# Attention with a prompt part on one core: whole copies of the Gram matrix, maxima ahead of a transpose, finishing pieces spread, another order at the end, and the prompt projection two stages later

## The chip, the cores and the metric

The kernel runs on one core of a Trainium2 chip. The metric is the device time of one execution in microseconds (us). Beside it there is one profiled execution, whose trace shows every instruction of the five engines: TensorE (PE, matmuls; PEld is its loading of weights), VectorE (DVE), ScalarE (ACT), GpSimd (POOL), and SyncE (SP), which in this kernel issues nearly all transfers. All times below are counted from the start of the profiled span.

## The reference

Eight batches of 112 queries attend to 375 context rows each: 371 rows of text and 4 of a prompt. There are 20 heads of 16 channels, and the context has 512 channels.

```python
q = heads(hidden_states @ W_q)                     # 8, 20, 112, 16
k_t, v_t = heads(text_ehs @ W_k), heads(text_ehs @ W_v)
probs_t = softmax(einsum('bhsd,bhtd->bhst', q, k_t) * Dh ** -0.5)
text_out = einsum('bhst,bhtd->bhsd', probs_t, v_t)
k_ip, v_ip = heads(ip_ehs @ W_k_ip), heads(ip_ehs @ W_v_ip)
attn_scores = einsum('bhsd,bhnd->bhsn', q, k_ip) * Dh ** -0.5
qsem = l2norm(einsum('bhst,bte->bhse', probs_t, text_ehs))
sem = einsum('bhse,bne->bhsn', qsem, l2norm(ip_ehs))
probs_ip = softmax(attn_scores + 0.5 * sem) * spatial_mask
ip_out = einsum('bhsn,bhnd->bhsd', probs_ip, v_ip)
out = (text_out + ip_out) @ W_out + b_out + hidden_states
```

The costly part is qsem: per batch and head a row of 371 probabilities times the context of 512 channels, of which only the length and four inner products are used.

## The kernel before, in words

**The idea.** The length of qsem comes from the Gram matrix G of the context, the inner products of all its rows: the squared length is p G p for a row p of (unnormed) probabilities. G is symmetric, so only the part above the diagonal is kept, doubled, with the diagonal halved. To the right of G stand the inner products with the prompt, a column of ones and the values of a head, so one chain of products p x [G, prompt, ones, values] gives all that a head needs.

**Steps.** A batch has five groups of four heads. A step is one group of one batch, 40 in all; `steps[n]` is the n-th. Four heads run beside each other, each in 32 rows of TensorE. Behind the first step (`alone`), the steps of the first seven batches go in pairs (n, n + 1) for odd n: `pair(n)` does the products of both, `behind(n + 1)` the TensorE work that belongs to other batches. Scores are two steps ahead (`LEAD`). The last batch has a loop of its own and then `ending`.

**One step.** `scores` (L681) makes the scores of a head in a PSUM bank. `probabilities` takes the maximum of each row on VectorE (L694, tile nmx), the exponential on ScalarE (L698, tile p), copies four prompt scores (L700, ipl), and has SP copy p into xg in the order that the transpose needs (L705). `transposed` turns xg with VectorE (L717) into xgT: a half takes six of the twelve blocks of 32 context rows, and the halves are separate instructions where a stage asks for them. `product` (L729) runs the twelve blocks; block j goes into the columns from 32 j on, so the chain gets shorter. The last blocks of the first step of a pair are mixed with the first block of the second. `reduced` (L782, VectorE) multiplies the result with p and sums, `value_sums` (L756, ScalarE) copies the rest.

**The Gram matrix.** `gram` (L501) makes G of a batch in three chunks of 128 context rows, in a PSUM bank each. The four column tiles p of TensorE take one block of 32 rows each; `DEAL[c]` says which block q tile p takes in chunk c, and block q starts at column 32 q, as the part left of it isn't needed. For each chunk there are four matmuls (e = 0..3) in each tile. `doubled` copies a chunk to the tile ug with ScalarE, times two: one instruction for the columns that all tiles have (L477) and three for what a tile has more (L481). GpSimd then multiplies 128 columns with a mask (L482) that has zeros, halves and ones; the masks follow `DEAL`. The first batch has another way, `first_gram`, with `doubled_whole`, one copy for a chunk. `gram_to_groups` has SP copy ug four times to the tile u of the batch (L515, four transfers for each of four blocks), `values_to_dram` and `values_to_groups` bring the values through DRAM to the tile vr (L591, L600), and `placed` copies the 64 value columns of a group into u with GpSimd (L647), three copies for a step, one for each chunk. The products of the next step wait for these.

**Buffers and queues that matter here.** The tile u has two buffers, for even and odd batches. The weights of the prompt (wip, L110) are loaded into a tile with the same tag, so that the u of batch 1 takes the place of wip. An engine works through its instructions in order, and so does SP's queue: a transfer that waits for its data or its place holds up all behind it. Pools with a `tag` give out buffers in turn.

**The prompt projection.** `prompt_projections` has three pieces: 32 short matmuls of all prompts with wip (L274), three ScalarE copies and one of GpSimd to the tile kv (L282 to L285); then three transposes of kv (L290), a copy to kip (L293) and three VectorE products to kipb (L295); then two transfers to vipd (L305). Before, the first piece lies in `behind(0)`, the second at the start of `behind(2)` and the third at its end.

**Finishing a batch.** `finish(b)` is a generator with pieces, which `f(b, n)` runs n at a time from the stages of the next two batches: (0) the largest of ss and a bound, (1) square root on ScalarE and 1/z, with `divided` on GpSimd, (2) the fused logits fu and their maxima (VectorE, L840 to L846), (3) their exponential (ScalarE, L850), (4) sums and the weights w (VectorE, L854 to L858), (5) the prompt's part wv on GpSimd (L864 to L871), (6) transposes of the result (TensorE L876, ScalarE L880), (7) the output product (L885) and its transfer. `ending` does the same for the last batch, which nothing hides, in smaller pieces (L898 on); the last batch's loop runs pieces of batch 6 (`before`) between its own.

**What sets the order.** TensorE, VectorE and SP follow the order in which the code issues instructions (`manual_schedule`); ScalarE's and GpSimd's instructions are placed by the scheduler in the main part.

## Time and profile before

| | us |
|---|---|
| runs, median of 3 | 417.56 |
| lowest and highest | 415.61, 419.80 |
| the profiled execution's own time | 415.55 |
| its span in the trace | 413.7 |
| TensorE's clock granted | 1.0 in all 40 slices |

The profiled execution lies 1.85 us above its span: that is what a launch adds around the traced instructions. It lies with the lowest of the three runs. A row of the timeline reads: start, duration, engine, line of the kernel, operation, tile written <- tiles read, shape, how many instructions are taken together; in brackets, the idle time of the engine before it and what ended that time. A row of a group reads: line, engine, operation, shapes, count, then busy time in us, the mean of one in ns, and the idle time ahead of it.

### The profile page before, as it was taken

To read this page: it belongs to the slowest core of one execution; us is meant where nothing else is said; L and a number is where in the kernel's file an instruction comes from. 1 tells how busy PE (TensorE), PEld (TensorE's weight loads), DVE (VectorE), ACT (ScalarE), POOL (GpSimd) and SP (SyncE) were. 2 spreads that over 40 slices of the span, in tenths; PEclk is the share of its full clock that TensorE was granted. 3 is DMA by queue.
4 is the path that set the end of the run, shared out by engine and by line. 5 is a ranking of instruction groups with operands and counts; after the bars stand their busy time and mean duration, and the time that the engine had idled before them with its cause. 6 is when DMAs were issued, how large, how long until landed. Compare 5 with 4: busy or idle time off the path is not lost.

```text
span 413.7 us, 14175 instructions
## 1 busy us (share of the span) xinstructions
PE 406.8 (98%) x5627; PEld 322.1 (78%) x5627; DVE 327.7 (79%) x700; ACT 199.3 (48%) x715; POOL 114.8 (28%) x271
## 2 busy tenths in 40 slices
PE   8999999999999999999999999999999999999996
PEld 7867777788778786879686877779787878687884
DVE  4256787877988877887898897897798897878975
ACT  3255342346443852535553664334733484336763
POOL 4203211121351351021170045002034126004671
PEclk9999999999999999999999999999999999999999
DMA  8877965976584846667676666566856344668320
GB/s 235 168 198 230 197 170 144 205 189 174 130 188 117 189 120 172 157 145 175 165 160 134 169 157 158 141 171 151 186 149 164 95 123 128 159 162 197 97 53 28
DMA packets 58244, 64.64 MB, mean 156 GB/s; under 512 B 19061, under 2 KB 52041, under 8 KB 58180
## 3 DMA queue, kind: packets, MB, share of 16 engines
q1 hardware_dynamic: 57150, 61.47, 61.0%
q0 software_dynamic: 464, 1.56, 1.6%
q8 instruction: 44, 0.72, 0.8%
q10 hardware_dynamic: 566, 0.72, 0.5%
q14 instruction: 20, 0.16, 0.1%
HBM read 19.03 MB, written 5.22 MB: 59 GB/s over the span
## 4 chain that ended last, share of the span: by engine, by line
PE 97%; POOL 1%; issue 0%; ACT 0%; DVE 0%; POOLq 0%
PE ps_qd L729 45%; PE ps_v L566 13%; PE ps_k L527 10%; PE ps_g L501 8%; PE ps_s L681 7%; PE ps_q L361 3%; PE ps_o L885 3%; PE ps_k L544 3%; PE ps_g L460 1%; PE ps_w L447 1%; PE ps_a L876 1%; PE ps_c L430 1%; PE ps_q L343 1%; PE ps_x L332 0%; PE ps_o L981 0%
## 5 line engine op out<-in xcount | busy, mean ns | idle before, releaser
L729 PE MATMUL ps_qd<-u,xgT 32*112 32x40 f32 (+11 forms) x3840 | 218.3, 352 | 1.1 <-POOL u L647 1.0
L729 PEld LDWEIGHTS ps_qd<-u,xgT 32*112 32x112 f32 x3840 | 181.4, 172 | 34.3 <-issue 5.5
L717 DVE STREAM_TRANSPOSE xgT<-xg 128x768 f32<-128x768 f32 (+1 forms) x63 | 123.4, 1977 | 10.4 <-DMA xg<-p 8.6
L698 ACT ACTIVATE p<-ps_s,nmx 112x371 f32<-112x371 f32 x160 | 86.0, 585 | 55.5 <-DVE nmx L694 54.1
L694 DVE TENSOR_REDUCE nmx<-ps_s 112x1 f32<-112x371 f32 x160 | 77.5, 536 | 32.9 <-PE ps_s L681 30.9
L647 POOL COPY u<-vr 128x64 f32<-128x64 f32 x120 | 26.9, 238 | 204.8 <-PE ps_qd L729 118.9
L782 DVE CUSTOM_DVE_ANT_0 p<-ps_qd,p 112x371 f32<-112x371 f32 x152 | 73.2, 536 | 12.9 <-ACT pvs L756 8.3
L681 PE MATMUL ps_s<-kT,qm 32*112 32x375 f32 (+1 forms) x320 | 62.0, 486 | 0.0
L566 PE MATMUL ps_v<-wv_sb,ctxT 128*128 128x320 f32 x192 | 56.1, 439 | 0.3 <-ACT kT L534 0.3
L756 ACT COPY pvs<-ps_qd 112x21 f32<-112x21 f32 x152 | 21.8, 197 | 55.7 <-DVE ss L782 49.2
L566 PEld LDWEIGHTS ps_v<-wv_sb,ctxT 128*128 128x128 f32 x192 | 35.3, 190 | 14.7 <-ACT kT L534 1.2
L527 PE MATMUL ps_k<-ctxT,wk_sb 128*128 128x371 f32 x128 | 43.6, 484 | 0.0
L527 PEld LDWEIGHTS ps_k<-ctxT,wk_sb 128*128 128x128 f32 x128 | 23.0, 190 | 13.2 <-issue 1.3
L681 PEld LDWEIGHTS ps_s<-kT,qm 32*112 32x112 f32 x320 | 28.5, 171 | 5.9 <-ACT ug L481 0.4
L501 PE MATMUL ps_g<-ctxT 128*32 128x375 f32 (+11 forms) x672 | 32.6, 334 | 0.0
L501 PEld LDWEIGHTS ps_g<-ctxT 128*32 128x32 f32 x672 | 27.9, 110 | 5.4 <-issue 2.0
L418 DVE STREAM_TRANSPOSE ctxT<-ct 128x512 f32<-128x512 f32 x21 | 22.2, 1069 | 6.1 <-DMA ct<-in_ctx_dram 6.1
L573 ACT COPY vext<-ps_v 128x320 f32<-128x320 f32 x24 | 10.2, 426 | 34.9 <-PE ps_v L566 33.9
L700 ACT COPY ipl<-ps_s 112x4 f32<-112x4 f32 x140 | 24.2, 173 | 0.0
L534 ACT COPY kT<-ps_k 128x371 f32<-128x371 f32 x16 | 7.5, 469 | 22.6 <-PE ps_k L527 22.3
L482 POOL TENSOR_TENSOR ug<-ug,half 128x128 f32<-128x128 f32 (+1 forms) x21 | 9.3, 450 | 30.7 <-ACT ug L481 30.7
L864 POOL TENSOR_TENSOR wv<-vip,w 112x1280 f32<-112x1280 f32 (+1 forms) x8 | 17.5, 2183 | 0.0
(153 smaller groups left out, 318.8 us busy)
## 6 DMA issues: line engine op xcount, KB each, us to landing
xg<-p SPq DMA_DIRECT2D x159, 162.3 KB
u<-ug SPq DMA_DIRECT2D x128, 99.0 KB
ct<-in_ctx_dram SPq DMA_DIRECT2D x28, 176.0 KB
vip<-vipd SPq DMA_DIRECT2D x7, 560.0 KB
vr<-vd SPq DMA_DIRECT2D x20, 120.0 KB
vd<-vext SPq DMA_DIRECT2D x7, 160.0 KB
out_dram<-ob SPq DMA_DIRECT2D x7, 140.0 KB
vr<-vd SPq DMA_DIRECT2D x12, 80.0 KB
```

What stands on the lines that cost most here:

```text
L418: nc.vector.transpose(ctxT[:, :, c * P : (c + 1) * P].rearrange("p e (j i) -> p j e i", i=RG), ct[:, some, :].rearrange("p j (k e) -> p j ...
L501: nc.tensor.matmul(ps[p * RG : (p + 1) * RG, q * RG : T - t0], ctxT[:, e, t0 + q * RG : t0 + (q + 1) * RG], ctxT[:, e, t0 + q * RG : T], s ...
L527: nc.tensor.matmul(ps[:, :TT], wk_sb[:, e, i * P : (i + 1) * P], s["ctxT"][:, e, :TT], start=(e == 0), stop=(e == NE - 1),)
L566: nc.tensor.matmul(ps[:, :C], ctxT[:, e, c * P : (c + 1) * P], wv_sb[:, e, :], start=(e == 0), stop=(e == NE - 1),)
L647: nc.gpsimd.tensor_copy(region(b, c)[:, :, UV - c * P :], s["vr"][:, c * QN : (c + 1) * QN, g, :])
L681: nc.tensor.matmul(ps[:S, :w], qm[a * RG : (a + 1) * RG, i, r, j * S : (j + 1) * S], s["kT"][a * RG : (a + 1) * RG, i, :w], start=True, st ...
L694: nc.vector.tensor_reduce(nmx, ps[:S, :TT], AX.X, ALU.max, negate=True)
L698: nc.scalar.activation(p, ps[:S, :TT], AF.Exp, bias=nmx)
L700: nc.scalar.copy(s["ipl"][:, groups[g][a], :], ps[:S, TT:T])
L717: nc.vector.transpose(xT[:, j : j + n].rearrange("p j (k q) -> p q j k", q=QN), xg[:, :, j * RG : (j + n) * RG].rearrange("p q (j k) -> p ...
L729: nc.tensor.matmul(banks[a][:S, j * RG : UW], xT[a * RG : (a + 1) * RG, j, :S], region(b, c)[a * RG : (a + 1) * RG, p, q * RG :], start=(j ...
L782: nc.vector.tensor_tensor_reduce(out=p, in0=ps[:S, :TT], in1=p, scale=1.0, scalar=0.0, op0=ALU.mult, op1=ALU.add, accum_out=s["ss"][:, h : ...
```

## The change

Five edits, in one diff.

1. *Whole copies.* `DEAL` gets other values for chunks 1 and 2. For batches 1, 2, 4 and 6 (`left_out` is false for their chunks 1 and 2) the matmuls of e = 0 in these chunks are made as wide as the chunk, and `doubled` then copies the chunk with one ScalarE instruction in place of four; what it copies more is zeroed by the mask. Chunk 0, and batches 3, 5 and 7, stay as they were, but for the dealing. The transfers of values to DRAM keep their number and change their sizes with the dealing.
2. *Maxima ahead.* In `pair(5)`, as in `pair(1)` before, the first half transpose of the second step comes behind the maxima of the coming step; `behind(4)` leaves it out.
3. *Finishing spread.* For odd batches, `behind` of group 1 runs pieces 1, 2 and 3 of `finish` at three places, and `pair` of group 2 runs 4 and 5. So fu and its maxima come ahead of the first half transpose on VectorE, and the sums and w, which came ahead of the next maxima, behind them.
4. *End order.* In the last batch's loop the scores for group 4 are issued one at a time after blocks 0 and 1, then two; pieces of batch 6's finish come at other places: GpSimd's first half of wv ahead of the shared products of group 2, both sums into attn ahead of the last batch's division, and TensorE's transposes of batch 6 ahead of those of batch 7.
5. *Prompt projection.* Its first piece moves from `behind(0)` to the start of `behind(2)`, which now runs it, the x transposes of `q`, the second piece, and then keys, half transpose, `q` and values. `behind(0)` makes two chunks of values in place of one, `behind(2)` one fewer.

Instructions: TensorE and SP have the same count of matmuls and transfers, ScalarE has 24 copies fewer.

```diff
--- before.py
+++ after.py
@@ -69,7 +69,7 @@
     assert (H, D, NC, NT, P) == (20, 16, 3, 3, 128) and RG == 2 * D
 
 
-    DEAL = ((0, 1, 2, 3), (3, 2, 0, 1), (1, 2, 3, 0))
+    DEAL = ((0, 1, 2, 3), (3, 1, 2, 0), (2, 3, 0, 1))
 
     def dealt(b, c):
         return DEAL[c] if b > 0 else DEAL[0]
@@ -465,15 +465,15 @@
                         stop=(e == NE - 1),
                     )
                 if c == NT - 1:
-                    doubled_whole(banks[r], r)
+                    doubled(banks[r], r, 0)
                 yield
 
-    def doubled(ps, c, deal=DEAL[0], h=0):
+    def doubled(ps, c, h, deal=()):
 
         t0 = c * P
         k = min(P, TT - t0)
         g = ug[:, GCOL[c] : GCOL[c] + T - t0]
-        common = (QN - 1) * RG
+        common = (QN - 1) * RG if deal else 0
         nc.scalar.mul(g[:, common:], ps[:, common : T - t0], 2.0)
         for p, q in enumerate(deal):
             if q < QN - 1:
@@ -481,13 +481,8 @@
                 nc.scalar.mul(g[own, q * RG : common], ps[own, q * RG : common], 2.0)
         nc.gpsimd.tensor_tensor(g[:, :k], g[:, :k], half[:, h, :k], ALU.mult)
 
-    def doubled_whole(ps, c):
-
-        t0 = c * P
-        k = min(P, TT - t0)
-        g = ug[:, GCOL[c] : GCOL[c] + T - t0]
-        nc.scalar.mul(g, ps[:, : T - t0], 2.0)
-        nc.gpsimd.tensor_tensor(g[:, :k], g[:, :k], half[:, 0, :k], ALU.mult)
+    def left_out(b, c):
+        return c == 0 or b > 1 and b % 2 == 1
 
     def gram(b):
 
@@ -498,14 +493,16 @@
             ps = bank(f"ps_g_{b}_{c}")
             for e in range(NE):
                 for p, q in enumerate(DEAL[c]):
+
+                    s0 = q * RG if e > 0 or left_out(b, c) else 0
                     nc.tensor.matmul(
-                        ps[p * RG : (p + 1) * RG, q * RG : T - t0],
+                        ps[p * RG : (p + 1) * RG, s0 : T - t0],
                         ctxT[:, e, t0 + q * RG : t0 + (q + 1) * RG],
-                        ctxT[:, e, t0 + q * RG : T],
+                        ctxT[:, e, t0 + s0 : T],
                         start=(e == 0),
                         stop=(e == NE - 1),
                     )
-            doubled(ps, c, DEAL[c], c)
+            doubled(ps, c, c, DEAL[c] if left_out(b, c) else ())
             yield
 
     def gram_to_groups(b, blocks):
@@ -1129,6 +1126,8 @@
 
     inputs = {7: (3, 5), 17: (5, B)}
 
+    late = (1, 5)
+
     def pair(n):
 
         one, two = steps[n], steps[n + 1]
@@ -1144,7 +1143,7 @@
                 coming_scores(n + LEAD, heads, tags[j])
                 coming_probabilities(n + LEAD, heads)
             if j == 1:
-                if n == 1:
+                if n in late:
                     transposed(*two, 0, BLK // 2)
                 transposed(*two, BLK // 2, BLK)
             if j % QN == QN - 1:
@@ -1168,7 +1167,7 @@
         if b % 2 and g in (0, NG - 1):
             f(b - 1 - (g == 0))
         if g in (1, 2):
-            f(b - 1, 3 - g)
+            f(b - 1, 2)
         reduced(b, g)
         value_sums(b, g)
 
@@ -1231,9 +1230,7 @@
             if n:
                 gr(nb, 2)
                 f(b - 1)
-            v(nb)
-            if n == 0:
-                run(("pp",), prompt_projections)
+            v(nb, 1 + (n == 0))
             if n:
                 tr(1)
                 f(b - 1, 2)
@@ -1244,11 +1241,16 @@
             turn[:] = ["qd"] * (6 + (b == 0)) + ["mm"]
             gram_to_groups(nb, (2,))
             if b == 0:
+                run(("pp",), prompt_projections)
+                q(nb, 3)
                 run(("pp",), None)
-            k(nb)
-            q(nb, 3)
-            tr(0)
-            v(nb)
+                k(nb)
+                tr(0)
+            else:
+                k(nb)
+                q(nb, 3)
+                tr(0)
+                v(nb)
             q(nb)
             v(nb)
             if b == 0:
@@ -1268,7 +1270,8 @@
             if b > 0:
                 f(b - 1)
             gr(nb + 1, 3)
-            tr(1)
+            if n + 1 not in late:
+                tr(1)
             if b > 0:
                 f(b - 1)
             load_next(b + 3)
@@ -1294,9 +1297,10 @@
             tr(0)
             f(b - 1)
             v(nb)
+            f(b - 1)
             tr(1)
             v(nb)
-            f(b - 1, 3)
+            f(b - 1)
             values_to_dram(nb, nc.sync, 0, 2)
             if b == B - 3:
                 prompt_values_by_head()
@@ -1350,7 +1354,7 @@
     places = {
         0: {0: (2, 3), 1: (0, 1)},
         1: {1: (3, 0), 2: (1, 2)},
-        2: {1: (0, 1), 2: (2, 3)},
+        2: {0: (0,), 1: (1,), 2: (2, 3)},
     }
     for g in range(NG):
         if g == 1:
@@ -1378,7 +1382,6 @@
                 next(sums)
             if g == 3 and j == 3:
                 placed(b, g + 1, (0,))
-                run(before, None)
                 transposed(b, g + 1)
                 drain(sums)
         if g == NG - 1:
@@ -1397,19 +1400,21 @@
             next(sums)
         elif g == 2:
             drain(held)
+            run(before, None)
         else:
             next(sums)
     drain(sums)
     last = ending(b, bd)
+    run(before, None)
     next(last)
+    value_sums(b, g, 1)
     run(before, None)
     reduced(b, g, 0, 1)
-    value_sums(b, g, 1)
     next(last)
     value_sums(b, g, 0, 1)
     reduced(b, g, 1)
     next(last)
-    run(before, None, 2)
+    run(before, None)
     next(last)
     next(last)
     run(before, None, 2)
```

## The prediction

> **What bounds the kernel now.** I read the page first (busy time, chain, groups), then TensorE's own timeline from one pair of steps to the next, because a busy share near the whole span says little about short stalls inside a group.
>
> ```profile
> PE 406.8 (98%) x5627; PEld 322.1 (78%) x5627; DVE 327.7 (79%) x700; ACT 199.3 (48%) x715; POOL 114.8 (28%) x271
> ...
> PE 97%; POOL 1%; issue 0%; ACT 0%; DVE 0%; POOLq 0%
> ...
> L729 PE MATMUL ps_qd<-u,xgT 32*112 32x40 f32 (+11 forms) x3840 | 218.3, 352 | 1.1 <-POOL u L647 1.0
> ```
>
> TensorE is busy in 406.8 us of the 413.7 us span and carries 97% of the chain; the products (L729) show only 1.1 us of idle time before them in all. So by the page the change, which removes no TensorE instruction, could win almost nothing. The page hides something, though: a matmul that waits after its weights are loaded counts as busy. The lengths of the pairs show it, each from its first product to the first matmul behind it.
>
> ```profile
> 46.00 1.22 PE L729 MATMUL ps_qd<-u,xgT 32*112 32x392 f32 x10
> ...
> 56.92 0.35 PE L290 MATMUL ps_kipT<-ident,kv 32*128 32x32 f32 x3
> ...
> 66.15 1.22 PE L729 MATMUL ps_qd<-u,xgT 32*112 32x392 f32 x10
> ...
> 85.86 1.22 PE L729 MATMUL ps_qd<-u,xgT 32*112 32x392 f32 x10
> ...
> 97.61 0.41 PE L343 MATMUL ps_q<-xT,wq_sb 128*64 128x112 f32 x4
> ...
> 106.58 0.60 PE L729 MATMUL ps_qd<-u,xgT 32*112 32x392 f32 x4
> ...
> 117.28 0.81 PE L566 MATMUL ps_v<-wv_sb,ctxT 128*128 128x320 f32 x2
> ...
> 203.44 1.22 PE L729 MATMUL ps_qd<-u,xgT 32*112 32x392 f32 x10
> ...
> 214.87 0.81 PE L566 MATMUL ps_v<-wv_sb,ctxT 128*128 128x320 f32 x2
> ```
>
> Pair(7), from 106.58 to 117.28, takes 10.70. Pair(1) takes 56.92 - 46.00 = 10.92, pair(5) 97.61 - 85.86 = 11.75, pair(17) 214.87 - 203.44 = 11.43. The work is the same, so pair(5) hides 1.05 us of stall and pair(17) 0.73. These are what the edits "maxima ahead" and "finishing spread" can reach.
>
> **The change part by part.**
>
> *Maxima ahead.* In pair(5) VectorE stands in front of a half transpose whose xg is still under way, with the next maxima behind it:
>
> ```profile
> 87.71 1.58 DVE L717 STREAM_TRANSPOSE xgT<-xg 128x768 f32<-128x768 f32 x1 [2.85 <-DMA xg<-p]
> ...
> 89.44 1.89 DVE L694 TENSOR_REDUCE nmx<-ps_s 112x1 f32<-112x371 f32 x4
> ...
> 108.86 1.89 DVE L694 TENSOR_REDUCE nmx<-ps_s 112x1 f32<-112x371 f32 x4
> ```
>
> The maxima start 89.44 - 85.86 = 3.58 us into the pair, against 108.86 - 106.58 = 2.28 in pair(7). With the first half transpose behind them, as pair(1) has it already, pair(5) should become as long as pair(1): 10.92 - 11.75 = -0.83. Bounds: 0 (xg lands so late that the transposes, now last, stall the second step instead) and -1.05. I take -0.83, since pair(1) is the same order of instructions.
>
> *Finishing spread.* In pair(17) the finishing of batch 2 stands ahead of the maxima:
>
> ```profile
> 206.37 0.30 DVE L858 SCALAR_TENSOR_TENSOR w<-ex,sm_sb,rx 112x80 f32<-112x80 f32 x1
> ...
> 206.71 1.90 DVE L694 TENSOR_REDUCE nmx<-ps_s 112x1 f32<-112x371 f32 x4
> ...
> 209.53 1.56 PEld L729 LDWEIGHTS ps_qd<-u,xgT 32*112 32x112 f32 x30 [0.26 <-ACT ipl L700]
> ```
>
> The maxima start 206.71 - 203.44 = 3.27 into the pair, 0.99 later than in pair(7), and at 209.53 TensorE waits for the banks that ScalarE's copies free. The new order puts the fu chain ahead of the half transpose and w behind the maxima, so about one microsecond of VectorE work leaves that place. Pair(17) falls to 10.70: -0.73 (bounds -0.73 and 0). Pair(7) and pair(27) have the same order but no such stall, so nothing comes there. The chain behind it has cover: ex, w and GpSimd's sums of that batch are needed a whole pair later.
>
> *Prompt projection moved.* TensorE's work stays:
>
> ```profile
> 42.42 2.42 PE L566 MATMUL ps_v<-wv_sb,ctxT 128*128 128x320 f32 x8
> ...
> 44.77 1.29 PE L274 MATMUL ps_kv<-wip,ipT 128*32 128x160 f32 x32
> ...
> 46.74 0.29 ACT L284 COPY kv<-ps_kv 64x160 f32<-64x160 f32 x1
> ...
> 59.79 0.74 PE L332 MATMUL ps_x<-ident,x_sb 112*128 112x112 f32 x6
> ...
> 102.19 4.47 PE L566 MATMUL ps_v<-wv_sb,ctxT 128*128 128x320 f32 x16
> ```
>
> Two chunks in a row cost 4.40 (106.58 - 102.19), in place of 46.00 - 42.42 = 3.58: pair(1) starts 0.82 later, at 46.82, and ends at 57.74; the projection's 1.23 follows, to 58.97, and one value chunk fewer makes it good. What is new is that the transposes of kv now follow the projection closely. They need two ScalarE copies of 0.29 (the copies start about 0.1 behind the matmuls) and GpSimd's copy of about as much, some 1.0 in all; the x transposes, 0.74 in between, cover most. I take +0.3 (bounds -0.1 and +1.0, no cover at all). The piece issues no transfer itself, and vipd stays in its place on SP; its copies move past the exponentials of pair(1) on ScalarE and past the first copies into u on GpSimd, and 0.9 us of ScalarE now stands ahead of kT, which is needed only when pair(3) begins.
>
> The dearer part is SP. The wip tile has the buffer that u_1 takes next, so the first copy into u_1 waits for the projection's last matmul. That stood at 46.0 and comes to 58.97. Behind that copy on SP stand xg of step 4, eight more copies of u, vipd, vd, xg of step 5, the values vr of batch 1, and xg of step 6.
>
> ```profile
> 53.06 2.49 SPq L515 DMA_DIRECT2D u<-ug  x4
> ...
> 56.39 3.63 SPq L705 DMA_DIRECT2D xg<-p  x4
> ...
> 60.08 5.03 SPq L515 DMA_DIRECT2D u<-ug  x8
> ...
> 76.35 2.90 SPq L600 DMA_DIRECT2D vr<-vd  x4
> ...
> 79.36 4.00 SPq L705 DMA_DIRECT2D xg<-p  x4
> ...
> 64.83 1.55 DVE L717 STREAM_TRANSPOSE xgT<-xg 128x768 f32<-128x768 f32 x1
> ...
> 67.74 1.90 DVE L694 TENSOR_REDUCE nmx<-ps_s 112x1 f32<-112x371 f32 x4 [1.36 <-PE ps_s L681]
> ...
> 84.62 0.59 POOL L647 COPY u<-vr 128x64 f32<-128x64 f32 x3 [5.17 <-DMA xg<-p]
> ```
>
> The first copy starts about 59.1 instead of 53.06, 6.0 late; the gap up to 56.39 takes 0.8 back, and from there the queue is almost without gaps, so everything stays 5.2 late. Two places feel it.
>
> First, xg of step 4 is issued until 60.02 + 5.2 = 65.2. A landing takes from 1.6 (the vr row at 128.95, below) to 4.3 (xg of step 6, from 83.36 to the transpose at 87.71, with the engines loaded), so the half transpose of 64.83 starts between 66.8 and 69.5 and the maxima behind it between 68.4 and 71.1. On time for a pair that starts at 66.2 would be 68.5 (pair(7)'s 2.28); pair(17) paid 0.73 for 0.99. So 0 to +2.3. I take +0.3, nearer the short landing, since the engines have had nothing from SP for six us by then.
>
> Second, vr. Its last issue ends at 79.25 and GpSimd starts its three copies at 84.62, the last instructions before pair(5) at 85.86; the slack is 85.86 - 85.21 = 0.65. What the delay does there depends on the landing:
>
> ```profile
> 124.24 3.10 SPq L600 DMA_DIRECT2D vr<-vd  x4
> ...
> 128.95 0.24 POOL L647 COPY u<-vr 128x64 f32<-128x64 f32 x1 [1.03 <-DMA vr<-vd]
> ...
> wo_sb<-in_L_xattn_W_out_dram POOLq DMA_DIRECT2D x1, 320.0 KB, 5.2
> ...
> bias_sb<-in_L_xattn_b_out_dram POOLq DMA_DIRECT2D x1, 140.0 KB, 5.8
> ```
>
> From 79.25 to the copies it took 5.4 us, behind GpSimd's loads of 0.5 MB; from 127.34 it took 1.6. After the change the last issue ends at 84.4. With 1.6 the copies end near 86.6 and pair(5), due at 86.2, waits 0.4; with 5.4 they end near 90.4 and it waits some 4.3. I take +0.4 (0 to +4.3): GpSimd's loads are issued behind pair(3)'s first step, near 72, land 5.2 to 5.8 later, and should be through by 79, before vr is issued at all.
>
> The Trainium skill, "DMA: Bandwidth & Descriptors", Queues, rings and completion order, says that each DMA engine takes turns between the queue rows that have work, a packet at a time. By that rule GpSimd's row stops costing SP's transfers as soon as its own packets are out, and the sum would be the one below; if instead the backlog were handed on in SP's row itself, the sum would be 4 us higher. The trace agrees as far as it goes: the same four vr copies take 5.4 with that load under way and 1.6 without.
>
> *Whole copies.* Four grams widen eight of their 48 matmuls, and ScalarE saves six copies in each.
>
> ```profile
> 31.78 4.65 PE L501 MATMUL ps_g<-ctxT 128*32 128x375 f32 x96
> ```
>
> By the widths in the code the longest of the four column tiles grows from 4904 columns (two passes) to 5032; at 4.65 us for 4904 that is at most 0.12 a gram, 0.5 for four. At least nothing, where another tile's turn set the end. I take +0.2. ScalarE is 48% busy, and the time that it wins is nobody's wait.
>
> *New end order.*
>
> ```profile
> 397.09 2.98 DVE L717 STREAM_TRANSPOSE xgT<-xg 128x768 f32<-128x768 f32 x2 [0.93 <-DMA xg<-p]
> ...
> 398.82 1.53 PE L729 MATMUL ps_qd<-u,xgT 32*112 32x392 f32 x16 [0.48 <-POOL u L647]
> ...
> 408.55 0.30 DVE L1001 SCALAR_TENSOR_TENSOR w<-ex,sm_sb,rx 112x80 f32<-112x80 f32 x1
> ```
>
> The last step's products start at 398.82, behind GpSimd's copies into u. GpSimd's first half of wv now runs earlier, so these copies come out of the way, but the first half transpose ends only at 397.09 + 1.49 = 398.58. So -0.2, not -0.48. Past the products the end is VectorE's chain to w, whose order stays; moving TensorE's ps_a and ps_o does not shorten it. Bounds -0.5 (xg earlier too) and +0.3 (more ahead of the copies on GpSimd).
>
> Sum: -0.83 - 0.73 + 0.3 + 0.3 + 0.4 + 0.2 - 0.2 = -0.56. The profiled execution took 415.55 us (span 413.7), so it would become 415.0. The runs shown have a median of 417.56 (415.61 to 419.80), 2.0 above that execution; on the median it is 417.0.
>
> **The rivals.**
>
> SP's queue decides (slower). If vr, delayed by 5.2, still meets a loaded set of DMA engines, it costs +4.3 at pair(5) and +0.7 at pair(3): +0.3 + 0.7 + 4.3 - 0.83 - 0.73 + 0.2 - 0.2 = +3.7, 421.3 on the median. It decides from the point where vr lands later than about 85.5 (copies 0.6, then the product at 86.2). With pair(3)'s +2.3 on top it would be 422.9. For it: the queue has no gaps to catch up in. Against it: with SP held, the engines empty.
>
> The spread does nothing (no change). The hidden stalls move to the transposes behind: in pair(5) xg of step 6, itself late by 5.2, lands near 89.5 to 91 and stalls the second step, and pair(17) trades a late maximum for a late transpose. Then -0.83 and -0.73 fall away: +1.0, 418.6.
>
> The end gives more (faster). If xg of the last step, issued one score earlier, frees the whole 0.93 us that VectorE waits at 397.09, and the projection's waits are covered: -0.83 - 0.73 - 0.9 + 0.4 = -2.1, 415.5. Against it: the last xg is issued by ScalarE, behind four exponentials whose places hardly move.
>
> **How the numbers follow.** Forecast 0.60, SP decides 0.15, spread does nothing 0.15, end gives more 0.10. The cases reach from -2.1 to +3.7 over 417.56, 415.5 to 421.3; the median of a few runs that lie 4 us apart adds a microsecond and a half below, where the profiled execution stood, and the upper part of the SP rival is left out. Range 414.0 to 420.6. One per cent is 4.2 us, about what a measurement of this kernel can tell from no change. No case by itself goes past it. Slower by over 1% needs the SP rival and a high draw: 0.06; faster, the end and a low draw: 0.06; within: 0.88.
>
> **What would show it.** Pair(5) at 10.9 with its maxima ahead of the half transpose; pair(17) at 10.7; SP's first copy into u_1 near 59 instead of 53; GpSimd's copies before pair(5) ending by 86.6; pair(3) not over 11.0; gram sections not over 4.7; the last products' start near 398 less what came before. Wrong would be a pair(5) that starts after 88, or a second step of pair(3) or pair(5) that waits on its transposes.

## The result, and the profile after

Over 22 runs each, side by side, the changed kernel takes 418.40 us and the kernel before 416.54; the ratio is 1.0042 (95% interval 1.0022 to 1.0063). By the ratio the change costs about 1.75 us (0.9 to 2.6) where a gain of 0.56 was forecast; by the medians it is 1.9. The three runs of before that the forecast had, with a median of 417.56, lay a microsecond high.

The page after the change (busy time, chain, the largest group):

```profile
PE 406.9 (98%) x5627; PEld 321.6 (77%) x5627; DVE 331.0 (79%) x700; ACT 194.8 (47%) x691; POOL 114.7 (28%) x271
...
PE 95%; DVE 2%; DMA 1%; ACT 0%; issue 0%; SPq 0%; POOL 0%; DVEq 0%; ACTq 0%; POOLq 0%
...
L726 PE MATMUL ps_qd<-u,xgT 32*112 32x40 f32 (+11 forms) x3840 | 217.7, 352 | 1.9 <-POOL u L644 1.3
```

TensorE has the same busy time as before, 406.9 us; VectorE has 3.3 us more with the same 700 instructions. Something on VectorE got slower without being more. The time before the products grew from 1.1 to 1.9 us, 1.3 of it for GpSimd's values. (Lines of the changed kernel are numbered three lower than before; L726 is the products.)

The span of the profiled execution is 416.6 us, 2.9 more than before. Part of that says nothing: the last two output transfers, the last rows of SyncE in either kernel, start at 410.55 before and 411.63 after.

```profile
411.63 0.80 SPq L1013 DMA_DIRECT2D out_dram<-ob  x2
```

From their end to the end of the span it is 416.6 - 412.43 = 4.2 us here and 413.7 - 411.34 = 2.4 in the kernel before. In the traces of the experiments it is 2.2 to 2.4, with the new end and with the old, but for e4 with 4.0. So 1.8 us of the 2.9 belong to that one execution. The lengths of the pairs tell more. They are read as in the prediction, from the first product of a pair to the first matmul behind it, here for all kernels at once (the Gram section is the 96 matmuls ahead of pair(5), to the pair's first product):

| kernel | pair(3) | Gram | pair(5) | pair(7) | pair(17) | pair(27) | ratio to before (95%) |
|---|---|---|---|---|---|---|---|
| before, as shown | 10.70 | 4.58 | 11.75 | 10.70 | 11.43 | 10.70 | 1 |
| before, second trace (e8) | 10.70 | 4.58 | 11.00 | 10.70 | 11.04 | 10.70 | 1 |
| changed | 10.94 | 5.94 | 11.51 | 11.29 | 11.37 | 11.35 | 1.0042 (1.0022-1.0063) |
| e1 old finishing | 10.96 | 5.63 | 11.67 | 11.67 | 10.70 | 11.57 | 1.0039 (1.0009-1.0068) |
| e2 old place of projection | 10.70 | 4.58 | 11.10 | 11.27 | 11.35 | 11.35 | 0.9979 (0.9952-1.0006) |
| e4 both of these | 10.70 | 4.58 | 11.07 | 11.24 | 10.70 | 10.70 | 0.9957 (0.9924-0.9991) |
| e9 SP's order | 10.70 | 4.58 | 11.41 | 11.45 | 11.35 | 11.41 | 1.0008 (0.9984-1.0031) |
| e10 1/z behind fu | 10.96 | 6.12 | 11.42 | 10.70 | 10.70 | 10.70 | 1.0002 (0.9978-1.0025) |
| e12 whole copies alone | 10.70 | 4.81 | 12.87 | 10.70 | 10.70 | 10.70 | 0.9988 (0.9958-1.0018) |
| e13 e9 and e10 | 10.70 | 5.52 | 11.62 | 10.70 | 10.70 | 10.70 | 0.9967 (0.9944-0.9990) |
| e14 e10, old place | 10.70 | 4.58 | 11.08 | 10.70 | 10.70 | 10.70 | 0.9950 (0.9922-0.9979) |

Of the pairs that the table leaves out, pair(15) and pair(19) differ most: 10.70 and 11.12 before, 11.23 and 10.70 in the changed kernel. Both move from trace to trace: pair(15) takes 10.70 to 10.84 in all experiments but e5 and e6, and pair(19) 10.70 in e8.

Two things went up in the changed kernel. First the way to pair(5): SyncE, GpSimd and TensorE, each from its own timeline.

```profile
58.00 2.50 SPq L512 DMA_DIRECT2D u<-ug  x4
60.60 3.63 SPq L702 DMA_DIRECT2D xg<-p  x4
...
81.42 2.16 SPq L597 DMA_DIRECT2D vr<-vd  x4
```

```profile
86.31 0.59 POOL L644 COPY u<-vr 128x64 f32<-128x64 f32 x3 [7.52 <-DMA xg<-p]
```

```profile
80.67 4.65 PE L498 MATMUL ps_g<-ctxT 128*32 128x375 f32 x96
86.61 1.22 PE L726 MATMUL ps_qd<-u,xgT 32*112 32x392 f32 x10 [1.28 <-POOL u L644]
...
92.17 2.15 PE L726 MATMUL ps_qd<-u,xgT 32*112 32x392 f32 x33 [0.28 <-DVE xgT L714]
```

SyncE stands still until the projection is done at 58.0; vr's last issue ends at 83.58 instead of 79.25; GpSimd starts its copies at 86.31 instead of 84.62; the products wait 1.28 us for them. xg of step 6, behind vr on the queue, is issued until 83.69 + 4.18 = 87.87, which is 1.3 us after pair(5) has begun; in the kernel before that was 83.36, or 2.5 us ahead of it. So the half transposes of pair(5), now last, wait for it, and the second step at 92.17 waits for them:

```profile
90.45 2.95 DVE L714 STREAM_TRANSPOSE xgT<-xg 128x768 f32<-128x768 f32 x2 [0.29 <-DMA xg<-p]
```

Second, VectorE in pair(7), which the forecast left out because it had no stall to lose. VectorE, then GpSimd, then TensorE:

```profile
105.82 0.75 DVE L839 TENSOR_TENSOR fu<-pvs,rn 112x80 f32<-112x80 f32 x1
106.60 0.79 DVE L840 SCALAR_TENSOR_TENSOR fu<-fu,ipl 112x80 f32<-112x80 f32 x1
...
107.87 1.57 DVE L714 STREAM_TRANSPOSE xgT<-xg 128x768 f32<-128x768 f32 x1
109.47 1.89 DVE L691 TENSOR_REDUCE nmx<-ps_s 112x1 f32<-112x371 f32 x4
...
114.20 0.30 DVE L855 SCALAR_TENSOR_TENSOR w<-ex,sm_sb,rx 112x80 f32<-112x80 f32 x1
114.42 0.54 DVE L779 CUSTOM_DVE_ANT_0 p<-ps_qd,p 112x371 f32<-112x371 f32 x1
```

```profile
105.73 0.74 POOL L822 TENSOR_TENSOR attn<-pvs,zr 112x320 f32<-112x320 f32 x1 [7.00 <-DVE zr L830]
106.43 0.86 POOL L793 TENSOR_TENSOR xb<-x_sb,bias_sb 112x320 f32<-112x320 f32 x1
```

```profile
107.09 1.22 PE L726 MATMUL ps_qd<-u,xgT 32*112 32x392 f32 x10
...
118.38 0.81 PE L563 MATMUL ps_v<-wv_sb,ctxT 128*128 128x320 f32 x2
```

VectorE in the same pair of the kernel before, and its two groups over the whole run, before and after (busy time, then the mean of one in ns):

```profile
104.87 1.57 DVE L717 STREAM_TRANSPOSE xgT<-xg 128x768 f32<-128x768 f32 x1
...
106.54 0.24 DVE L842 TENSOR_TENSOR fu<-pvs,rn 112x80 f32<-112x80 f32 x1
106.82 0.24 DVE L843 SCALAR_TENSOR_TENSOR fu<-fu,ipl 112x80 f32<-112x80 f32 x1
...
113.04 0.51 DVE L782 CUSTOM_DVE_ANT_0 p<-ps_qd,p 112x371 f32<-112x371 f32 x1
```

```profile
L843 DVE SCALAR_TENSOR_TENSOR fu<-fu,ipl 112x80 f32<-112x80 f32 x7 | 2.8, 399 | 0.2
L842 DVE TENSOR_TENSOR fu<-pvs,rn 112x80 f32<-112x80 f32 x7 | 2.6, 377 | 0.2
```

```profile
L840 DVE SCALAR_TENSOR_TENSOR fu<-fu,ipl 112x80 f32<-112x80 f32 x7 | 5.0, 708 | 0.2
L839 DVE TENSOR_TENSOR fu<-pvs,rn 112x80 f32<-112x80 f32 x7 | 3.6, 518 | 0.2
```

Two operations that took 0.24 us each in this pair take 0.75 and 0.79, and the two groups together 8.6 us in place of 5.4: nearly all of VectorE's 3.3 us. Each ends 0.10 us behind an operation of GpSimd that runs beside it: 106.47 and 106.57, then 107.29 and 107.39. The sums of the products start at 114.42, 7.33 us into the pair, behind w (before: 113.04 - 106.58 = 6.46); ScalarE's copies that free the banks wait for them, and TensorE's next scores for these copies. The waits have a row that the kernel before did not have:

```profile
PEld ps_s L678 <- ACT pvs L753: 1.7, 6, 0.4
```

The kernel before had the same effect at other places. In the finishing of an odd batch it reads, on VectorE and on GpSimd:

```profile
241.42 0.80 DVE L843 SCALAR_TENSOR_TENSOR fu<-fu,ipl 112x80 f32<-112x80 f32 x1
```

```profile
241.24 0.87 POOL L796 TENSOR_TENSOR xb<-x_sb,bias_sb 112x320 f32<-112x320 f32 x1
```

It ends at 242.22, GpSimd's at 242.11. The means of 377 and 399 ns in the groups before, where an operation alone takes 240, were the sign of it, and the forecast did not use them.

### The profile page after: what moved, and what is told of

It is laid out like the page before. It is cut to its first block, busy times and chain, and to the rows that moved or that the text cites. A ratio compares the mean times of both kernels' runs of the same rounds, so it can differ in the third digit from the quotient of the medians.

```text
span 416.6 us, 14143 instructions
## 1 busy us (share of the span) xinstructions
PE 406.9 (98%) x5627; PEld 321.6 (77%) x5627; DVE 331.0 (79%) x700; ACT 194.8 (47%) x691; POOL 114.7 (28%) x271
## 4 chain that ended last, share of the span: by engine, by line
PE 95%; DVE 2%; DMA 1%; ACT 0%; issue 0%; SPq 0%; POOL 0%; DVEq 0%; ACTq 0%; POOLq 0%
PE ps_qd L726 45%; PE ps_v L563 13%; PE ps_k L524 10%; PE ps_g L498 8%; PE ps_s L678 7%; PE ps_q L361 3%; PE ps_k L541 3%; PE ps_o L882 2%; PE ps_g L460 1%; DMA xg<-p 1%; PE ps_w L447 1%; PE ps_q L343 1%; PE ps_c L430 1%; DVE p L779 0%; PE ps_a L873 0%
## 5 line engine op out<-in xcount | busy, mean ns | idle before, releaser
L726 PE MATMUL ps_qd<-u,xgT 32*112 32x40 f32 (+11 forms) x3840 | 217.7, 352 | 1.9 <-POOL u L644 1.3
L726 PEld LDWEIGHTS ps_qd<-u,xgT 32*112 32x112 f32 x3840 | 180.9, 172 | 34.1 <-issue 6.4
L498 PE MATMUL ps_g<-ctxT 128*32 128x119 f32 (+11 forms) x672 | 32.4, 338 | 0.0
L482 POOL TENSOR_TENSOR ug<-ug,half 128x128 f32<-128x128 f32 (+1 forms) x24 | 10.6, 447 | 31.2 <-ACT ug L481 26.1
```

What stands on the lines that cost most here:

```text
L498: nc.tensor.matmul(ps[p * RG : (p + 1) * RG, s0 : T - t0], ctxT[:, e, t0 + q * RG : t0 + (q + 1) * RG], ctxT[:, e, t0 + s0 : T], start=(e ...
L726: nc.tensor.matmul(banks[a][:S, j * RG : UW], xT[a * RG : (a + 1) * RG, j, :S], region(b, c)[a * RG : (a + 1) * RG, p, q * RG :], start=(j ...
```

## The experiments

All but e8 and e12 are the changed kernel with the edit shown. Theory A: the loss is SyncE's held queue and the spread finishing. Theory B, the rival: it lies at the end of the kernel. C, the rival of e3, e5 and e9, is another cause for the loss ahead of pair(5). Later D and E, two causes inside the spread.

**e1, the old finishing.**

```diff
-            f(b - 1, 2)
+            f(b - 1, 3 - g)
...
             v(nb)
-            f(b - 1)
             tr(1)
             v(nb)
-            f(b - 1)
+            f(b - 1, 3)
```

> The changed kernel with the finishing of even batches as it was before the change (pieces 1, then 2, 3 and 4 in a row behind group 1, piece 5 in the pair). Theory A: the changed kernel is slower for two reasons, SP held behind u_1 (about 1.3 us at the start of pair(5), 0.2 in pair(3), 0.6 left inside pair(5)) and the spread of the finishing (pair(7) and pair(27) went from 10.70 to 11.29 and 11.35). Then here pair(7) and pair(27) return to 10.70 and pair(17) goes back to about 11.4, while the 1.3 us ahead of pair(5) stays: 0.7 to 1.2 us faster than the changed kernel, ratio to the kernel before about 1.001 to 1.003. Theory B: the loss is at the end of the kernel (new end order, the last output lands 1.9 us later), and the pairs do not count: the ratio stays at 1.004.

A miss: 1.0039, only 0.1 us won. Pair(17) is at 10.70, but pair(7) at 11.67 and pair(27) at 11.57. In the old order the half transpose stands ahead of fu, w and the maxima, and here it found its xg late:

```profile
107.34 1.57 DVE L714 STREAM_TRANSPOSE xgT<-xg 128x768 f32<-128x768 f32 x1 [0.97 <-DMA xg<-p]
```

In the kernel before it did not wait (104.87 above, no bracket). So the old order has a cost too, when transfers are late, and they are late in this kernel. With an interval of 0.3% on either side the ratio can't tell whether 0.1 us or 1 was won.

**e2, the old place of the projection.**

```diff
-            v(nb, 1 + (n == 0))
+            v(nb)
+            if n == 0:
+                run(("pp",), prompt_projections)
...
-                run(("pp",), prompt_projections)
-                q(nb, 3)
...
+            k(nb)
+            q(nb, 3)
+            tr(0)
+            v(nb)
```

> The changed kernel with the prompt projection's first piece and the value chunk back in their old places. Theory A: the first copy into u_1 is issued near 53 again, GpSimd's copies of values end before the Gram section does, so the wait of 1.28 us at the start of pair(5) goes, pair(3) is 10.70 again, and pair(5), now with its maxima ahead, takes about 10.9 in place of 11.51: 1.5 to 2.3 us faster than the changed kernel, ratio to before 0.998 to 1.001. Pair(7) and pair(27) stay at 11.3. Theory B: ratio stays at 1.004, since the end is the same.

0.9979, 2.6 us better than the changed kernel; pair(3) and the Gram section are back at 10.70 and 4.58. Theory B is out: the end is the new one here. What the forecast had not seen comes to light in the old place: the projection waits for its weights. Here 0.52 us, in e7 1.05, in e14 1.59, and in e4:

```profile
46.85 1.28 PE L274 MATMUL ps_kv<-wip,ipT 128*32 128x160 f32 x28 [1.92 <-DMA wip<-in_L_xattn_W_v_ip_dram]
```

In these four the projection is reached 5.7 to 6.9 us after SyncE has begun to issue the second half of wip, in the two traces of the kernel before 7.1 and 7.6. The weights are there 7.6 to 8.2 us after that issue; in e12, where the projection is reached after 6.6, they were there in time. So the wait comes of the earlier arrival, which the whole copies bring, and of a landing that differs from trace to trace.

**e3 and e5, the weights in other tiles.** In e3 three quarters of one matrix lay in the tile of the output weights; a memset of that tile's padding comes later and zeroes a part of them, so that its numbers are not those of the kernel. Its memset also held GpSimd up. e5, shown here, avoids both.

```diff
-    wip = work.tile([P, UCOL], F32, tag="u", name="wip")
+    wvip = work.tile([P, NE * C], F32, tag="vip", name="wvip", bufs=1)
+    wkx = work.tile([P, 2 * C], F32, tag="xb", name="wkx", bufs=1)
...
-    load_embed(nc.sync, wkip_sb, w_k_ip)
+    wk_parts = w_k_ip.rearrange("(p e) f -> p e f", e=NE)
+    nc.sync.dma_start(wo_sb[:, :FULL, :], wk_parts[:, :FULL, :])
+    nc.sync.dma_start(wkx.rearrange("p (e f) -> p e f", f=C), wk_parts[:, FULL:, :])
```

> The changed kernel with the prompt's weights in other tiles (one half in the place that the tile kv takes later, the other in the tiles of the output weights and of xb), so that u_1 no longer waits for the projection; the projection stays in its new place. One transfer more in the prologue. Theory A, with the wait on the shared buffer as the mechanism: SP issues the first copy into u_1 near 52 to 53, the 1.28 us ahead of pair(5) and the 0.2 in pair(3) go, as in the run with the old place: 1.3 to 2.1 us faster than the changed kernel. Rival C: it is the order on TensorE and ScalarE (the copies of kv and the later transposes) that costs, then the time stays near that of the changed kernel and only SP's start moves.

> The changed kernel with the prompt's weights in tiles that u_1 does not take (half in the place of the output weights' first two chunks and of xb, half where kv comes later); the projection stays in its new place. Unlike in the run before it, no memset on GpSimd has to wait for these weights. Theory A, the wait on the shared buffer: SP issues the first copy into u_1 near 53 instead of 58, the products of pair(5) do not wait for values, pair(3) takes 10.70, and the time falls by 1.3 to 2.1 us against the changed kernel, ratio to the kernel before 0.998 to 1.001, as with the old place (0.9979). Rival C, the order on TensorE and ScalarE around the moved projection: SP starts early, but less than 0.7 us is won.

1.0046 (1.0013 to 1.0079) and 1.0028 (0.9995 to 1.0061). Neither time tells the theories apart: in both, xg of step 2 came late behind the split loads, and pair(1) took 14.8 and 15.1 us in the traces (11.02 in the changed kernel), so that SyncE's first copy into u_1 stood at 58 all the same.

```profile
52.69 2.91 DVE L715 STREAM_TRANSPOSE xgT<-xg 128x768 f32<-128x768 f32 x2 [2.37 <-DMA xg<-p]
```

What lies behind pair(1) speaks for theory A. The copy no longer waits for the projection: in e5 it starts ahead of the projection's first matmul, in the changed kernel behind its last one.

```profile
57.58 2.49 SPq L513 DMA_DIRECT2D u<-ug  x4
```

```profile
61.88 0.33 PE L275 MATMUL ps_kv<-wo_sb,ipT 128*32 128x160 f32 x2
```

And with the projection still in its new place on TensorE and ScalarE, pair(3) takes 10.70, the Gram section 4.58, and pair(5) 11.06 (e3) and 11.13 (e5). It is no clean test, as the long pair(1) gives SyncE time as well.

**e4, both undone (e1 and e2).**

> The changed kernel with both undone, the spread of the finishing and the place of the projection; whole copies, maxima ahead in pair(5) and the new end order remain. Theory A: the two costs add, 2.3 to 3.3 us faster than the changed kernel, and with pair(5) at 10.9 about 0.5 to 1 us faster than the kernel before (ratio 0.9975 to 0.9995). Theory B: ratio 1.004, as the end order is still the new one.

0.9957 (0.9924 to 0.9991): 3.5 us better than the changed kernel, and faster than the kernel before. Pair(7) stays at 11.24, as in e1: its half transpose waits 0.53 us for xg.

**e6 and e7, GpSimd's operations written behind fu** (e7 with the projection in its old place).

```diff
         nc.vector.reciprocal(zr, z)
-        divided()
...
+        def on_gpsimd():
+            divided()
...
         nc.vector.tensor_tensor(fu, fu, over_ip(mx), ALU.subtract)
+        if not (b % 2 or b == B - 2):
+            on_gpsimd()
```

> The changed kernel with GpSimd's two operations of the finishing (divided and xb) of batches 0, 2 and 4 issued behind the fu chain instead of ahead of it. Theory D: in the changed kernel the first two fu operations take 0.75 and 0.79 us in place of 0.24 because GpSimd's attn and xb run at the same time (they lie side by side with them in pair(7), pair(17), pair(27)); this puts the half transpose, the maxima and the reductions 1.06 us back. Then here all fu operations take 0.24 and pair(7), pair(17), pair(27) fall from 11.3 to 10.7 or nearly: about 1.5 us faster than the changed kernel, ratio about 1.0005. Rival E: not the two operations but sx, rx and w, which now stand ahead of the sums of the products, are the delay; then fu falls to 0.24 and the pairs stay near 11.3 less at most a third of a microsecond.

> The changed kernel with the projection in its old place and GpSimd's two operations behind the fu chain: whole copies, maxima ahead, spread finishing and the end order remain. If theories A and D hold, no pair but (1), (5) and perhaps (15), (19), (25) is over 10.7, and the kernel is 3 to 4 us faster than the changed one, ratio to the kernel before 0.993 to 0.996, as fast as the run with both edits undone (0.9957) or faster. If rival E holds it stays near 0.998.

1.0030 (1.0003 to 1.0058) and 0.9984 (0.9965 to 1.0004); pairs at 11.2 to 11.4. This was no test: GpSimd waits for 1/z alone, so it started beside fu as before, and fu still took 0.75 and 0.78. In the main part `manual_schedule` names ScalarE and GpSimd too, so GpSimd keeps the order of the code; but nothing else of GpSimd's stands between the old place and the new. Writing an operation later does not make another engine do it later.

**e8, the kernel before once more.**

> The kernel before once more, for a second trace of it. If pair(5), pair(17), pair(19) and pair(25) are 11.75, 11.43, 11.12 and 11.17 again, these stalls belong to the order of the instructions; if one of them is 10.70 here, that stall depends on the run, and no edit can be credited with its absence.

Pair(5) takes 11.00 in place of 11.75, pair(17) 11.04 in place of 11.43, pair(19) 10.70 in place of 11.12; pair(25) stays, with 11.13 in place of 11.17. The order is the same; in pair(5) what differs is how late xg lands:

```profile
86.40 1.58 DVE L717 STREAM_TRANSPOSE xgT<-xg 128x768 f32<-128x768 f32 x1 [2.04 <-DMA xg<-p]
```

2.04 us of waiting here, 2.85 in the trace of the prediction, and 4.28 in e12, where SyncE issues xg later, too, and pair(5) takes 12.87 (the bracket names the transfer that ended last by the profile, there another one):

```profile
88.27 1.58 DVE L714 STREAM_TRANSPOSE xgT<-xg 128x768 f32<-128x768 f32 x1 [4.28 <-DMA ct<-in_ctx_dram]
```

**e9, SP's order mended.**

```diff
-            if g in (1, 2):
-                gram_to_groups(nb, (g - 1,))
+            if g in (1, 2) and (b or g == 2):
+                gram_to_groups(nb, (g - 1,) if b else (0, 1))
```

> The changed kernel with one change of order on SP: the first block's copies into u_1 are issued behind xg of step 4, together with the second block's, so that xg of step 4 no longer stands behind the wait for the projection. No other engine's order changes. Theory A (the queue behind that wait is what costs): SP copies xg of step 4 between about 54 and 58, in the time in which it now stands still, the values vr are issued some 3.6 us earlier (near 78), and the products of pair(5) do not wait for GpSimd's copies; the Gram section before pair(5) takes 4.6 in place of 5.9, pair(3) 10.7, pair(5) 11.0 to 11.1: 1.5 to 2.1 us faster than the changed kernel, ratio to the kernel before 0.999 to 1.0005. Rival C: the wait at pair(5) stays, because values or xg are held up by the load on the transfer engines and not by the queue's order: ratio stays near 1.004.

1.0008: 1.4 us better. SyncE issues xg of step 4 from 56.68 on, in place of 60.60, the values 1.5 us earlier than in the changed kernel (3.6 were expected), and the wait at pair(5) is gone (5.94 to 4.58):

```profile
51.07 9.11 SPq L702 DMA_DIRECT2D xg<-p  x8
60.27 7.60 SPq L512 DMA_DIRECT2D u<-ug  x12
...
79.92 2.15 SPq L597 DMA_DIRECT2D vr<-vd  x4
```

```profile
81.08 4.65 PE L498 MATMUL ps_g<-ctxT 128*32 128x375 f32 x96
85.67 1.22 PE L726 MATMUL ps_qd<-u,xgT 32*112 32x392 f32 x10
```

So it is the queue's order that costs; rival C, by which the wait stays, is out for this run. The wait is gone in e11 and e15 too, which have the same order on SP; in e13's trace, of an execution 2.0 us above that kernel's median, the values come late again:

```profile
87.34 1.22 PE L726 MATMUL ps_qd<-u,xgT 32*112 32x392 f32 x10 [0.86 <-POOL u L644]
```

Inside pair(5) the gain stayed out (11.41). xg of step 6 is issued until 82.18 + 3.66 = 85.84, still 0.2 us after the pair has begun, and the half transposes wait for it; in e4, where it is issued 0.9 us ahead of the pair, they do not:

```profile
89.41 2.95 DVE L714 STREAM_TRANSPOSE xgT<-xg 128x768 f32<-128x768 f32 x2 [0.25 <-DMA xg<-p]
```

```profile
91.30 2.96 DVE L714 STREAM_TRANSPOSE xgT<-xg 128x768 f32<-128x768 f32 x2
```

**e10, 1/z behind fu**, so that GpSimd has something to wait for.

```diff
-        nc.vector.reciprocal(zr, z)
-        divided()
...
+        def on_gpsimd():
+            nc.vector.reciprocal(zr, z)
+            divided()
...
         nc.vector.tensor_tensor(fu, fu, over_ip(mx), ALU.subtract)
+        if not (b % 2 or b == B - 2):
+            on_gpsimd()
```

> The changed kernel with 1/z of batches 0, 2 and 4 made behind the fu chain on VectorE, so that GpSimd's two operations, which need it or stand behind it, cannot run beside fu (in the run before they were only written later and still ran beside it). Theory D: all fu operations take 0.24, the half transpose, the maxima and the sums of the products come 1.06 us earlier, pair(7), pair(17) and pair(27) take 10.7: 1.5 to 1.9 us faster than the changed kernel, ratio 0.9995 to 1.001. Rival E: sx, rx and w ahead of the sums are enough to hold the banks: fu takes 0.24, and the pairs stay at 11.1 to 11.3.

1.0002: 1.7 us better, and pair(7), pair(17) and pair(27) all at 10.70. VectorE and GpSimd in pair(7):

```profile
106.59 0.24 DVE L844 TENSOR_TENSOR fu<-pvs,rn 112x80 f32<-112x80 f32 x1
106.87 0.24 DVE L845 SCALAR_TENSOR_TENSOR fu<-fu,ipl 112x80 f32<-112x80 f32 x1
...
114.54 0.54 DVE L779 CUSTOM_DVE_ANT_0 p<-ps_qd,p 112x371 f32<-112x371 f32 x1
```

```profile
107.92 0.74 POOL L822 TENSOR_TENSOR attn<-pvs,zr 112x320 f32<-112x320 f32 x1 [8.28 <-DVE zr L832]
```

The sums start 114.54 - 108.01 = 6.53 us into the pair, as early as in the kernel before (6.46). sx, rx and w still stand ahead of them, so rival E is out: the two long operations were the whole of what these three pairs lost. The Trainium skill, "SBUF — State Buffer", 🔬 SBUF: two separate sides, says that VectorE and GpSimd share one pair of ports, and that an operation of VectorE with two inputs in SBUF and one of GpSimd that reads SBUF take it in turns, each for its whole length. The trace agrees: 0.24 us apart, 0.75 and 0.79 beside GpSimd, ending 0.10 behind it.

**e11, e1 and e9 together; e12, whole copies alone in the kernel before.**

> The changed kernel with the old finishing and the new order on SP, the projection in its new place: what should remain of the change when both costs are out. If theories A and E or D hold it is as fast as the run with both edits undone (0.9957) or faster, because there the projection in its old place waited 1.0 to 2.4 us for the load of its weights (its 32 matmuls took 2.2 to 3.6 us in three runs, 1.2 in the kernel before): 0.993 to 0.997.

> The kernel before with the whole copies and the new dealing alone. In every run that has them the products ahead of the first value chunk took 5.36 in place of 6.06, 0.70 us less, which the forecast did not have; the other Gram sections took 4.53 in place of 4.58. If nothing else follows: 0.8 us faster than before, ratio 0.998. Rival: the projection, now 0.7 us earlier, waits for its weights as it did in the runs with the old place: ratio 0.999 to 1.003.

0.9980 (0.9953 to 1.0006), less than expected: pair(5) 11.60, pair(7) 11.14, the old order with late transfers again. And 0.9988: 0.5 us better, not clear of noise; here the projection did not wait (1.30), but pair(5) did, 12.87.

**e13, e9 and e10 together; e14, e10 with the projection in its old place; e15, e13 with the old end order.**

> The changed kernel with both repairs: 1/z behind the fu chain, and xg of step 4 ahead of the copies into u_1 on SP. If the two costs add and are the whole loss: pair(3), pair(7), pair(17), pair(27) at 10.7, no wait for values at pair(5), pair(5) at 11.1 to 11.6, pair(1) 11.0: about 3.2 us faster than the changed kernel, ratio to the kernel before 0.995 to 0.998. If something else carries the loss: 0.999 or more.

> The changed kernel with 1/z behind the fu chain and the projection in its old place. Pairs as in the run before, pair(5) nearer 11.1, but the projection waits for its weights (2.2 to 3.6 us for its 32 matmuls in place of 1.2): ratio 0.995 to 0.998 too. If the weights' load is what matters, it is slower than the run with SP's order mended by 0.5 to 1.5 us; if the load on SP and the transfer engines around pair(3) and pair(5) matters more, faster.

> As the run with both repairs, but with the old end order of the last batch. The forecast gave the new end order 0.2 us. From the traces so far the stretch from the first product of group 1 of the last batch to the end of the last transposes differs by under 0.3 us between kernels with the old and with the new order, both ways: the ratio is within 0.001 of the run with both repairs.

0.9967, 0.9950 and 0.9964 (0.9936 to 0.9993). e9 won 0.0034 and e10 0.0040 against the changed kernel; together they win 0.0075. That the sum fits so closely is luck, as each gain is known to about 0.003 (1.3 us); but the two costs add as far as that shows, and without them the rest of the change is a gain. e14 has the best ratio of all, 2.1 us under the kernel before, though its projection waited 1.59 us for its weights in the trace; its interval and e13's overlap. e15 differs from e13 by 0.0003: the end order neither gives nor takes anything that can be seen.

## Why the prediction was wrong, point by point

- *Finishing spread, -0.73.* This step failed, by sign. It counted the instructions that leave one place of VectorE, and not what runs beside the place they go to: GpSimd's attn and xb, which start as soon as 1/z is there. Measured, pair(17) -0.06, pair(7) +0.59, pair(27) +0.65, +1.2 in all, and e10 puts the cost at 1.7 us. Part of the stall that was to be won was not the order's either: pair(17) of the same kernel took 11.04 in e8. "The same order but no such stall, so nothing comes there" was the sentence that hid it: a pair without a stall has nothing to win and something to lose.
- *Maxima ahead, -0.83.* Not shown as a gain; the trace has -0.24. The stall of pair(5) belongs to the landing of xg and moved between 11.00, 11.75 and 12.87 in three traces without the edit. With it, pair(5) took 11.06 to 11.13 in the six traces in which xg of step 6 is issued ahead of the pair (e2, e4, e7, e14, and e3 and e5), and 11.41 to 11.76 in the eight in which the issue ends 0.2 to 1.6 us after the pair has begun; there the transposes wait 0.21 to 0.62 us. That is the bound of 0 that the step itself named, transposes that stall the second step; the forecast reckoned with an xg 5.2 us late and still took the gain whole. One trace's 11.75 was taken for a property of the order.
- *Values behind SyncE's queue, +0.4 (0 to +4.3).* The mechanism was right, the size was off: +1.36 on the Gram section. The first copy came at 58.0 (59.1 was forecast), and the landing took neither 1.6 nor 5.4 us but 86.31 - 83.58 = 2.7. xg of step 4 in pair(3): +0.24, as taken (+0.3).
- *Projection's copies, +0.3.* From the first value chunk to pair(3) it was 66.15 - 42.42 = 23.73 before and is 65.30 - 41.13 = 24.17 after:

```profile
41.13 4.57 PE L563 MATMUL ps_v<-wv_sb,ctxT 128*128 128x320 f32 x16
...
58.95 0.37 PE L290 MATMUL ps_kipT<-ident,kv 32*128 32x32 f32 x3 [0.28 <-ACT kv L284]
...
65.30 0.93 PE L726 MATMUL ps_qd<-u,xgT 32*112 32x392 f32 x8
```

  +0.44. What the step left out is what the old place can cost: a wait of 0.5 to 1.9 us for wip in e2, e4, e7 and e14, none in e12.
- *Whole copies, +0.2.* Wrong by sign. The wider matmuls cost nothing that shows: the Gram sections that wait for nothing take 4.58 as before. And the step before the first value chunk took 42.42 - 36.37 = 6.05 before and takes 41.13 - 35.77 = 5.36, 0.69 less, in every trace with whole copies; e12, which has nothing else, shows it too. What stands there on ScalarE is the copies of batch 1's Gram matrix, and TensorE's next scores waited for the last of them, 0.43 us in the trace of the kernel before and 0.42 in e8; no trace with whole copies has that row. How the rest of the 0.69 comes about is not shown. "The time that it wins is nobody's wait" did not hold at that place.

```profile
36.37 0.93 PE L729 MATMUL ps_qd<-u,xgT 32*112 32x392 f32 x8
```

```profile
37.73 0.17 PEld L681 LDWEIGHTS ps_s<-kT,qm 32*112 32x112 f32 x1 [0.43 <-ACT ug L481]
```

```profile
35.77 1.22 PE L726 MATMUL ps_qd<-u,xgT 32*112 32x392 f32 x10
```

- *End order, -0.2.* Nothing to be seen (e13, e15).

The SP rival had the place and the sign right; it was forecast as the lesser case, and at +3.7 in all. Its cost was 1.4 us (e9). The overlap on VectorE was in no rival, and cost 1.7 (e10). With either one mended the change comes to about zero (1.0008 with SyncE's order, 1.0002 with 1/z moved), so it took both to make it a loss. Left open: why the values came late in e13's trace alone, why the landing of xg and wip differs between executions, and how much of the gain of e14 is each remaining edit's; no run separates the edits there.

## What to carry to other kernels

When an operation moves on one engine, look at what another engine does at the place it moves to: here 0.24 us became 0.75 and 0.79, and no row calls it a wait, only a longer duration. A group whose mean lies above the time of one instruction alone is a place to look. When work moves past a shared buffer, follow the queue of whoever waits for that buffer down to its last transfer, and see whether something behind it could go first; here two lines gave 1.4 us back. And a stall that ends with a transfer's landing should be seen in two traces before it is priced.

## What was not expected of the hardware

VectorE's operation on 112x80 values, 0.24 us alone, took 0.75 and 0.79 us beside two operations of GpSimd. The half transposes beside the same operations of GpSimd took no longer than elsewhere: 1.57 us at 104.87 in the kernel before. The landing of the same transfer moved much between executions of one program: xg ahead of pair(5) was waited for 2.04 and 2.85 us. And the last output's issue ended 2.2 to 2.4 us before the end of the span in fifteen traces, 4.0 and 4.2 in two, with the same end of the code in both groups.
